# Layer 0 of a two-layer attention block: output product over two rows by seven products, inverses spread by transfers, gate by tanh

## The chip, the cores and the metric

The kernel runs on one core of one Trainium2 chip. The metric is the device time of one execution in microseconds (us). Everything is computed in fp32.

The engines are named as in the profile: PE (TensorE, the matmuls; PEld is its loading of the stationary operand), DVE (VectorE), ACT (ScalarE), POOL (GpSimd) and SP (SyncE, which here only issues DMA transfers). PE writes to PSUM, eight banks of 512 fp32 columns on 128 partitions.

## The reference

Two layers, each of which normalizes its input by groups of channels and adds an attention to it. The input `x` is 1 x 128 x 256 x 256: 128 rows (`S`), in each 256 places (`R`) with 256 channels (`C`). The change is in layer 0, whose core is:

```python
gate = sigmoid(msa_repr @ gate_proj)                       # msa_repr = gn(x)
q, k, v = split(msa_repr @ qkv_proj, 3)                    # 8 heads of 32 channels
sim = softmax(einsum('nsqhc,nskhc->nshqk', q, k) * 32 ** -0.5)
sim = sim + bias                                           # bias from pair_repr, the same for all rows
attend = einsum('nshqk,nskhc->nsqhc', sim, v) * gate
x = x + attend @ out_proj
```

Attention runs inside each of the 128 rows. Layer 1 is a banded attention with 4 heads of 64 channels; `x` between the layers is kept in DRAM (`x1`). The statistics that layer 1's normalization needs are gathered while layer 0 produces its rows.

## The kernel before, in words

Channels lie on the partitions, in two halves of 128. A tile of one row is [128, 2 halves, 256 places]. An early stage of some 190 us loads `x` for the statistics, turns the pair tensor into `bias_sb` and prepares weights. Layer 0 is then one loop over the rows `s`. Layer 1 follows.

**Two rows at a time by seven products.** Two rows times two halves of channels against a 2 x 2 block of weights would be eight products of 128 x 128 by 256 columns. `Seven` does it with seven, in Strassen's manner: `Quarters` holds the sums of weight quarters, `row_sums` (on POOL) makes sums of the normalized rows in `ts`, and the products are added on top of each other inside a PSUM bank, so that a half bank must be read between two products: product 7 is added to the half bank after ACT has copied it (`take("6")`), and product 4 after `take("7")`. q, k, v and g (the gate's input) of two rows are made this way. `two_of_them` runs two of them interleaved: q and k in an even iteration, v and g in an odd one. A product is four matmuls on strips of 32 columns of the array, and each of these has two records in the trace.

**The output product** is done row by row with all eight products per two rows: `one_by_one` yields after each of its four products per row, and `two_of_them` takes one from this generator (`next(po, None)`) behind product 7 of the first, one behind product 4 of the first, and the other two at the end. In iteration `s` it works on row `s - 1`.

**One iteration `s`** (the text calls it even or odd by `s`), in the order of the program:

- `scores(s, 0)`: scores of the first four heads into four banks, four exponentials on ACT (`ex`);
- `sum_heads(s - 1)`: the softmax totals `zs` of the row before, as products of ones with `both` (the sum of both halves of the keys, added by `join_tiles` on DVE), a head's total lying on 32 partitions, 512 columns in all; then `bv`, the product of bias and values;
- `divide(s - 1)`: ACT copies `zs` to `z` (and adds it up in `zsum`), DVE makes `d = (g + 1) * z` and its reciprocal. `g` holds exp(-gate input), made by ACT in every even iteration for two rows;
- `attend(s - 1)`: `av`, the product of exponentials and values; on DVE `t = bv * z`, `t = av + t`, `at = t * d`;
- `scores(s, 1)`, three exponentials, then `stretch`: the two `Seven` with the output product between them, and the fourth exponential behind the first copy;
- the remaining joins, `least` (the minimum of `z`), `normal(s + 4)` (transposes and normalizes a later row), `sum_rows` in odd iterations, `finish(s - 1)` (adds `xt` to the output product, statistics, the store of two rows).

PE, ACT and DVE run in exactly this order in layer 0 (a manual schedule); POOL and SP are ordered by the planner.

**PSUM.** Five of the eight banks are one ring for scores, `Seven`, `two` and the output product; a new use takes the bank that was given back longest ago. `zs`, `bv` and `av` have one bank each.

**Layer 1** makes its output product by seven already (`Summed`) and spreads its inverses by transfers: `by_transfer` writes them to DRAM (`rz_far`) and reads them back broadcast over partitions (`near`).

Of the kernel before, what the change touches and what calls it, by code (L numbers as in the profile page):

```python
# [15 lines left out]
P = 128  # L16
# [23 lines left out]
def conv_preact_kernel(  # L40
# [103 lines left out]

    w_out_t = const.tile([P, 2, C], F32, name="w_out_t")
# [35 lines left out]
    quarters["g"] = Quarters(const, gate_sb, 0, "g")  # L181

# [178 lines left out]
    with ExitStack() as early:  # L361
# [10 lines left out]
        def load_weights():  # L372
            w_raw = pr_pool.tile([P, 8, C], F32, tag="pr", name="w_raw")
            nc.gpsimd.dma_start(out=w_raw[:, 6:8, :], in_=out_w.rearrange("(t p) c -> p t c", p=P))
            nc.gpsimd.dma_start(out=w_raw[:, 0:6, :], in_=w_in.rearrange("(t p) c -> p t c", p=P))
            nc.gpsimd.dma_start(out=w_nat[:, 6:8, :], in_=w_out.rearrange("(t p) c -> p t c", p=P))
            nc.gpsimd.dma_start(out=b_raw[0:6], in_=b_in.rearrange("(t p) -> t p", p=P))
            nc.gpsimd.dma_start(
                out=b_raw[6:8].rearrange("h (a r) -> h a r", a=A),
                in_=b_out.rearrange("(a h r) -> h a r", a=A, h=2),  # L380
            )
            for h in range(2):
                cols = slice(h * P, (h + 1) * P)
                for to, t0, t1 in ((out_sb, 6, 8), (w_nat, 0, 6)):
                    nc.gpsimd.tensor_copy(
                        to[:, 0 : t1 - t0, cols].rearrange("p t (a r) -> p t a r", a=A),
                        w_raw[:, t0:t1, :].rearrange("p t (a h r) -> p t h a r", a=A, h=2)[:, :, h],
                    )
# [177 lines left out]
    def row_sums(t, x, engine):  # L566

        engine.tensor_tensor(t[:, 0], x[:, 2], x[:, 0], ALU.subtract)  # L568
        engine.tensor_tensor(t[:, 1], x[:, 3], t[:, 0], ALU.subtract)
        engine.tensor_tensor(t[:, 2], x[:, 3], x[:, 2], ALU.subtract)  # L570
        engine.tensor_tensor(t[:, 3], x[:, 1], t[:, 1], ALU.subtract)
# [51 lines left out]
    def two_of_them(pool, f, g, name, po, rest=lambda: None):  # L623


        for p in (f, g):
            p.open()
            p.product(1)
            p.product(5)
            p.take("15")  # L630
            if p is f:
                rest()
        twos = proj_bank(f"p2{name}")
        two = pool.tile([P, 2, R], F32, tag="two", name=f"two{name}", bufs=1)
        f.product(2, twos[:, 0, :], first=True)
        g.product(2, twos[:, 1, :])
        nc.scalar.copy(two, twos)  # L637
        for p in (f, g):
            p.product(3)
            p.product(6)  # L640
            p.take("6")

        for n, what in ((7, "7"), (4, "34")):
            f.product(n)
            f.take(what)
            next(po, None)
            g.product(n)
            g.take(what)
        for _ in po:
            pass  # L650
        for n, p in enumerate((f, g)):
            p.add_two(two[:, n, :])
            p.add_mid()
# [41 lines left out]

    def in_turn(sevens, amid=lambda n: None):


        for p in sevens:
            p.open()  # L700

            p.product(2, p.ps[:, 1, :], first=True)
            p.take(2)
        for n in (1, 5, 6, 7, 4, 3):
            for p in sevens:
                p.product(n)
                p.take(n)
            if n in (1, 5):
                amid(n)
# [22 lines left out]
    with ExitStack() as both:  # L732
# [6 lines left out]
        ygs = {}  # L739
        rz_far = dram.tile([2, 2, 4, R], F32, name="rz_far")  # L740

        def load1(g):
            if g * XG < S and g not in ygs:

                if g % 7 < 2:
                    yg = big.tile([P, XG * (R // B), C // A], F32, tag="xg", name=f"yg{g}")
                    yg = yg.rearrange("p n c -> p (n c)").rearrange("p (s h q) -> p s h q", h=2, q=R)
                else:
                    yg = big1.tile([P, XG, 2, R], F32, tag="yg", name=f"yg{g}", bufs=5)
                nc.sync.dma_start(out=yg, in_=rows(x1, g * XG, XG))  # L750
                ygs[g] = yg

        with ExitStack() as lay0:
# [6 lines left out]
            xns, tss, res = {}, {}, {}  # L760

            def normal(s):
# [5 lines left out]
                xt = row.tile([P, 2, R], F32, tag="xt", name=f"xt{s}", bufs=6)  # L768
# [63 lines left out]
            def sum_heads(s):  # L832
# [4 lines left out]
                for half in range(2):  # L837
                    both = hd[s, half][1]
                    for j in range(4):
                        nc.tensor.matmul(  # L840
                            zs[D0 * j : D0 * (j + 1), half, :], lhsT=ones[:, 0:D0], rhs=both[:, j, :],
                            start=True, stop=True,
# [5 lines left out]
            def divide(s, zs):  # L848
                if s < 0:
                    return  # L850
                i, r = divmod(s, 2)
                z = att.tile([P, 2, R], F32, tag="z", name=f"z{s}", bufs=1)
                nc.scalar.activation(z, zs, AF.Identity, accum_out=zsum[:, s : s + 1])
                d = att.tile([P, 2, R], F32, tag="d", name=f"d{s}", bufs=1)
                nc.vector.scalar_tensor_tensor(d, res["g", i][:, 2 * r : 2 * r + 2, :], 1.0, z, op0=ALU.add, op1=ALU.mult)
                nc.vector.reciprocal(d, d)  # L856
                hd[s, "z"] = (z, d)

            def least(s, z):
                if s >= 0:  # L860
                    nc.vector.tensor_reduce(zmin[:, s : s + 1], z, axis=AX.XY, op=ALU.min)

            def attend(s):
# [5 lines left out]
                z, d = hd.pop((s, "z"))  # L869
                t = att.tile([P, 2, R], F32, tag="t", name=f"t{s}", bufs=1)  # L870
                nc.vector.tensor_tensor(t, bv0, z, ALU.mult)  # L871
                nc.vector.tensor_tensor(t, av, t, ALU.add)
                at = row.tile([P, 2, R], F32, tag="at", name=f"at{s}", bufs=1)
                nc.vector.tensor_tensor(at, t, d, ALU.mult)  # L874
                st[s]["at"] = at

            def finish(s):
                if s < 0:
                    return
                po = st[s]["po"]  # L880
                g, k = divmod(s, XG)
                if k == 0:
                    outs[g] = big1.tile([P, XG, 2, R], F32, tag="o", name=f"o{g}")
                o = outs[g]
                nc.vector.tensor_tensor(o[:, k], po, st[s]["xt"], ALU.add)
                first, part = (k, S // 2 - 1 + k) if s >= S - 2 else (k - 1, s // 2)
                if first == k or k == 1:
                    for half in range(2):
                        nc.vector.bn_stats(out=stats1[:, half, part, :], in_=o[:, first : k + 1, half, :])
# [3 lines left out]
                st.pop(s)  # L893

            def stretch(names, i, s, rest=lambda: None):

                po = iter(())
                if s >= 0:
                    po = one_by_one(out_sb, st[s]["at"], f"po{s}", lambda ps: st[s].update(po=ps), B)
                if 2 * i >= S:  # L900
                    rest()
                    for _ in po:
                        pass
                    return
# [8 lines left out]
            with tc.manual_schedule(engines={mybir.EngineType.PE, mybir.EngineType.Activation, mybir.EngineType.DVE}):  # L913
# [3 lines left out]
                stretch("qk", 0, -1)  # L917
                for s in range(2, 4):
                    normal(s)
                stretch("vg", 0, -1)  # L920
                sum_rows(1)
                most1 = Most(st1, stats1, 3, 1)
                for s in range(S):
                    scores(s, 0)()
                    zs = sum_heads(s - 1)
                    join_tiles(s, 0, 0)
                    divide(s - 1, zs)
                    if s % 2 == 0:
                        e = res["g", s // 2]
                        nc.scalar.activation(e, e, AF.Exp, scale=-1.0)  # L930
                    z = hd[s - 1, "z"][0] if s > 0 else None
                    rest = ((0, 2), (1, 0), (1, 2))
                    if s < S - 1:
                        attend(s - 1)
                        last_exp = scores(s, 1)
                        if s == 4:
                            for weights in quarters1.values():
                                weights.sum()
                        stretch(("qk", "vg")[s % 2], s // 2 + 1, s - 1, last_exp)
                        for half, j in rest:  # L940
                            join_tiles(s, half, j)
                        least(s - 1, z)
                        if s >= S - 3:
                            most1.join(s - S + 3)
                        normal(s + 4)
                        if s % 2 == 1:
                            sum_rows((s + 3) // 2)
                        finish(s - 1)
                    else:

                        scores(s, 1)()
                        for half, j in rest:
                            join_tiles(s, half, j)
                        least(s - 1, z)
                        attend(s - 1)
# [11 lines left out]
                attend(S - 1)  # L967
                for s in (S - 2, S - 1):
# [12 lines left out]
        with ExitStack() as lay:  # L981
            ps_av = psum(lay, "1", 4, 0)
            row = lay.enter_context(tc.tile_pool(name="row1", bufs=4))
# [368 lines left out]
    with tc.If(sure < P):  # L1352
        with ExitStack() as lay:
# [69 lines left out]
            def again(layer, s, mean, rstd):  # L1423
# [38 lines left out]
                if layer == 0:  # L1462
# [5 lines left out]
                    nc.vector.tensor_tensor(at, at, e, ALU.mult)  # L1468
# [64 lines left out]
```

## Time and profile before

| What | Value |
|---|---|
| Time, median of 3 runs | 3140.39 us (3139.83 to 3141.06) |
| The profiled execution's own time | 3144.71 us |
| Its span, first to last instruction | 3142.9 us |
| Granted PE clock, mean | 0.993 |
| PE busy | 3062.3 us, 97% |
| DVE busy | 2542.5 us, 81% |
| ACT busy | 1869.8 us, 59% |
| POOL busy | 1623.3 us, 52% |
| Layer 0 in the trace | from about 190 us to about 2065 us |

The profile is of one execution, so its durations are to be compared with its own time; the median of the runs is 4.3 us lower. Engines overlap, so the shares do not add up. A line such as `L577` is a line of the kernel; `out<-in` names the tiles; `[idle <- X]` is how long the engine stood before the instruction, and what released it. In the answer by stretches, each line has the stretch, its length, then busy time (and instructions) of PE, PEld, DVE, ACT and POOL, the granted clock, the DMA share and GB/s.

### The profile page before, as it was taken

How to read it: one execution, taken by the hardware profiler on the slowest of the kernel's cores; microseconds unless marked ns; L12 is line 12 of the kernel's file. 1: busy time of each engine (PE TensorE's matmuls, PEld its weight loads, DVE VectorE, ACT ScalarE, POOL GpSimd, SP SyncE). 2: the span in 40 equal slices, each digit the busy share in tenths (PEclk: the TensorE clock that was granted, in tenths of full speed). 3: DMA queues.
4: the chain of work that ended last, by engine and by line, in shares of the span. 5: the costliest groups of instructions: out<-in, count | busy, mean ns of one | idle time of the engine just before them, and what ended most of it. 6: DMA issues, size and time to landing. Idle time of an engine off the chain costs nothing.

```text
span 3142.9 us, 135072 instructions
## 1 busy us (share of the span) xinstructions
PE 3062.3 (97%) x60161; PEld 2030.7 (65%) x60161; DVE 2542.5 (81%) x4140; ACT 1869.8 (59%) x4064; POOL 1623.3 (52%) x1651
## 2 busy tenths in 40 slices
PE   6889999999999999999999999999999999999997
PEld 4556666566666656666665666567777777777775
DVE  4669999999999999999999999956666666666665
ACT  4666666666666666666666666645555555555553
POOL 3034444444444444444444444347677777777774
PEclk9999999999999999999999999999999999999999
DMA  9941111111111111111111111004444444444443
GB/s 376 424 122 42 44 43 36 43 37 41 38 36 43 36 43 37 42 37 36 43 36 43 37 41 38 30 29 103 100 100 103 95 98 104 101 99 102 95 99 70
DMA packets 357293, 245.47 MB, mean 78 GB/s; under 512 B 276072, under 2 KB 342112, under 8 KB 350560
## 3 DMA queue, kind: packets, MB, share of 16 engines
q1 hardware_dynamic: 355808, 234.39, 27.4%
q8 instruction: 474, 7.77, 1.1%
q0 software_dynamic: 752, 2.36, 0.2%
q14 instruction: 115, 0.94, 0.1%
q10 hardware_dynamic: 144, 0.00, 0.0%
HBM read 169.09 MB, written 67.62 MB: 75 GB/s over the span
## 4 chain that ended last, share of the span: by engine, by line
PE 91%; DMA 5%; DVE 2%; ACT 1%; issue 0%; POOL 0%; SPq 0%; DVEq 0%; POOLq 0%; ACTq 0%
PE sim L794 8%; PE po L577 7%; PE av L826 7%; PE bv L826 7%; PE p1v L1055 7%; PE p1q L577 6%; PE p1o L577 6%; PE p1k L577 6%; PE pv L577 6%; PE pq L577 6%; PE pk L577 5%; PE pg L577 5%; DMA pr<-in_L_conv_pair_repr_dram 4%; PE zs L840 4%; PE 1sim L1076 3%; PE 1av L1117 3%
## 5 line engine op out<-in xcount | busy, mean ns | idle before, releaser
L807 ACT ACTIVATE ex<-sim 128x512 f32<-128x512 f32 x1024 | 547.6, 605 | 422.4 <-PE sim L794 422.4
L816 DVE TENSOR_TENSOR both<-ex 128x512 f32<-128x512 f32 x512 | 487.7, 991 | 69.1 <-ACT ex L807 68.9
L856 DVE RECIPROCAL d<-d 128x512 f32<-128x512 f32 x128 | 429.2, 3353 | 4.4
L618 POOL TENSOR_TENSOR v<-v,twovg 128x256 f32<-128x256 f32 x64 | 78.4, 1224 | 544.4 <-ACT twovg L637 544.4
L577 PE MATMUL po<-at,out_sb 128*32 128x256 f32 x4096 | 291.6, 381 | 4.1 <-DVE at L874 4.1
L794 PE MATMUL sim<-q,k 32*64 32x256 f32 x8192 | 288.3, 387 | 1.2 <-ACT ex L807 1.2
L826 PE MATMUL bv<-bias_sb,v 128*32 128x256 f32 x4096 | 244.5, 379 | 0.7 <-DVE t L871 0.7
L826 PE MATMUL av<-ex,v 128*32 128x256 f32 x4096 | 244.5, 379 | 0.0
L1086 POOL TENSOR_TENSOR 1p<-1ex,seen 128x768 f32<-128x768 f32 x127 | 231.8, 1825 | 13.0 <-ACT 1ex L1084 13.0
L1055 PE MATMUL p1v<-w_in_t,1xn 128*64 128x128 f32 x4096 | 236.4, 273 | 0.3 <-POOL place L990 0.3
L1055 PEld LDWEIGHTS p1v<-w_in_t,1xn 128*64 128x64 f32 x4096 | 231.6, 137 | 6.0 <-POOL place L990 0.6
L677 ACT ACTIVATE 1q<-p1q,bqk 128x256 f32<-128x256 f32 x192 | 91.1, 474 | 242.5 <-PE p1q L577 126.4
L794 PEld LDWEIGHTS sim<-q,k 32*64 32x64 f32 x8192 | 152.1, 131 | 126.8 <-issue 79.2
L618 POOL TENSOR_TENSOR q<-q,twoqk 128x256 f32<-128x256 f32 x64 | 51.8, 810 | 290.7 <-ACT twoqk L637 290.7
L1186 DVE TENSOR_TENSOR 1at<-1av,1near 128x512 f32<-128x512 f32 x128 | 82.5, 686 | 143.2 <-DMA 1near<-rz_far 124.2
L826 PEld LDWEIGHTS bv<-bias_sb,v 128*32 128x32 f32 x4096 | 133.2, 110 | 88.7 <-issue 1.1
L826 PEld LDWEIGHTS av<-ex,v 128*32 128x32 f32 x4096 | 133.2, 110 | 87.9 <-issue 0.4
L577 PEld LDWEIGHTS po<-at,out_sb 128*32 128x32 f32 x4096 | 131.2, 110 | 70.8 <-issue 4.7
L1093 POOL TENSOR_TENSOR 1zp<-1p 128x512 f32<-128x512 f32 x127 | 162.4, 1279 | 10.0
L568 POOL TENSOR_TENSOR 1ts<-1xn 128x256 f32<-128x256 f32 x64 | 46.8, 732 | 230.6 <-ACT 1xn L1016 230.6
L775 DVE TENSOR_SCALAR xn<-xt,mean,rstd 128x256 f32<-128x256 f32 x256 | 160.8, 667 | 0.0
L334 DVE BATCH_NORM_STATS2 stats<-xs 128x6 f32<-128x128 f32 x512 | 100.3, 277 | 65.1 <-DMA xs<-in_x_dram 65.1
(300 smaller groups left out, 7599.0 us busy)
## 6 DMA issues: line engine op xcount, KB each, us to landing
pr<-in_L_conv_pair_repr_dram SPq DMA_DIRECT2D x32, 1024.0 KB
xs<-in_x_dram SPq DMA_DIRECT2D x16, 2048.0 KB
x<-o SPq DMA_DIRECT2D x64, 512.0 KB
yg<-x SPq DMA_DIRECT2D x64, 512.0 KB
out_dram<-1o SPq DMA_DIRECT2D x256, 128.0 KB
xg<-in_x_dram SPq DMA_DIRECT2D x252, 128.0 KB
1near<-rz_far SPq DMA_DIRECT2D x124, 256.0 KB
rz_far<-1rz SPq DMA_DIRECT2D x124, 4.0 KB
```

Source lines behind the costliest of these rows:

```text
L577: nc.tensor.matmul(out[cols], lhsT=lhsT[:, cols], rhs=rhs, **flags)
L618: nc.gpsimd.tensor_tensor(self.to[:, 0], self.to[:, 0], two, ALU.add)
L775: nc.vector.tensor_scalar(xns[i][:, 2 * r + half, :], xt[:, half, :], mean0[:, half : half + 1], rstd0[:, half : half + 1], op0=ALU.subtra ...
L794: nc.tensor.matmul(sims[j][KB * c : KB * (c + 1), kt, :], lhsT=k[p0 : p0 + D0, 2 * r + half, k0 : k0 + KB], rhs=q[p0 : p0 + D0, 2 * r + ha ...
L807: nc.scalar.activation(ex[:, j], sims[j], AF.Exp, scale=1.0 / math.sqrt(D0))
L816: nc.vector.tensor_tensor(both[:, j : j + 2], ex[:, j : j + 2, 0, :], ex[:, j : j + 2, 1, :], ALU.add)
L826: nc.tensor.matmul(to[D0 * j : D0 * (j + 1), half, :], lhsT=v[:, 2 * r + half, c0 : c0 + D0], rhs=weights(4 * half + j, kt), start=(kt == ...
L840: nc.tensor.matmul(zs[D0 * j : D0 * (j + 1), half, :], lhsT=ones[:, 0:D0], rhs=both[:, j, :], start=True, stop=True,)
L856: nc.vector.reciprocal(d, d)
L1055: nc.tensor.matmul(ps[KB * half : KB * (half + 1), b, :], lhsT=xns[i][:, 2 * r + kt, KB * b : KB * (b + 1)], rhs=w_in_t[:, kt, 2 * C + P * ...
L1086: engine.tensor_tensor(p.rearrange("p j (r c) -> p (j r) c", c=WROW)[:, :, 0 : 2 * WSTEP] .rearrange("p r (t c) -> p r t c", c=WSTEP)[:, : ...
L1093: engine.tensor_tensor(zp, p[:, :, 0:R], p[:, :, R : 2 * R], ALU.add)
```

## The change

- The output product of layer 0 goes over two rows by seven products (`Output`, a `Summed`). It works on rows `s - 3` and `s - 2` in odd iterations `s`; even iterations have none. Its operand `at` is kept for two rows, POOL makes the row sums (`out_sums`), and DVE takes each product's result, adding `xt` on the way. `two_of_them` asks for the output products at more places.
- The totals of both halves of the heads are packed into 256 columns (16 partitions each, by `place0`). DVE takes the reciprocal of these 256 columns. One transfer writes eight partitions of it to DRAM, four read it back, each broadcast over 32 partitions (`near`). The last row does this by two products with `spread0` instead.
- The row's result is `at = (tanh + 1) * (av * near + bv)` in three DVE steps (`gated`), at the end of an even iteration, and between the takes of the output product in an odd one; `av` and `bv` stay in PSUM until then. ACT makes tanh of half the gate's input where it made the exponential, and `out_sb` is halved when it is loaded.
- The order in an iteration: the fourth exponential of the first heads comes behind `divide`; `join_tiles(s, 0, 2)`, `least` and `normal(s + 4)` come before `scores(s, 1)`.
- `row_sums` does two of its four subtractions in one instruction (in both layers). `xt` has eight buffers instead of six; layer 1's `yg` buffers are allocated only in layer 1.

```diff
     def row_sums(t, x, engine):
-        engine.tensor_tensor(t[:, 0], x[:, 2], x[:, 0], ALU.subtract)
+        engine.tensor_tensor(t[:, 0::2], x[:, 2:4], x[:, 0::2], ALU.subtract)
         engine.tensor_tensor(t[:, 1], x[:, 3], t[:, 0], ALU.subtract)
-        engine.tensor_tensor(t[:, 2], x[:, 3], x[:, 2], ALU.subtract)
         engine.tensor_tensor(t[:, 3], x[:, 1], t[:, 1], ALU.subtract)
...
-        for p in (f, g):
-            p.product(3)
-            p.product(6)
-            p.take("6")
-
-        for n, what in ((7, "7"), (4, "34")):
-            f.product(n)
-            f.take(what)
-            next(po, None)
-            g.product(n)
-            g.take(what)
+        f.product(3)
+        next(po, None)
+        f.product(6)
+        f.take("6")
+        next(po, None)
+        g.product(3)
+        next(po, None)
+        g.product(6)
+        g.take("6")
+        f.product(7)
+        f.take("7")
+        next(po, None)
+        g.product(7)
+        g.take("7")
+        f.product(4)
+        f.take("34")
+        next(po, None)
+        g.product(4)
+        g.take("34")
         for _ in po:
             pass
...
+    class Output(Summed):
+        WIDTH = B
...
+        def out(self, to, half, m, r):
+            nc.vector.tensor_tensor(to, self.ps[:, half, :], self.y[r][:, m], ALU.add)
+
+        def stream(self, amid=()):
+            amid = iter(amid)
+            self.open()
+            for n in (2, 1, 5, 6, 7, 3, 4):
+                if n == 2:
+                    self.product(2, self.ps[:, 1, :], first=True)
+                else:
+                    self.product(n)
+                self.take(n)
+                next(amid, lambda: None)()
+                yield
...
                     for j in range(4):
                         nc.tensor.matmul(
-                            zs[D0 * j : D0 * (j + 1), half, :], lhsT=ones[:, 0:D0], rhs=both[:, j, :],
-                            start=True, stop=True,
+                            zs[strip(j), 0, :], lhsT=place0[:, half, :], rhs=both[:, j, :],
+                            start=(half == 0), stop=(half == 1),
                         )
...
-                z = att.tile([P, 2, R], F32, tag="z", name=f"z{s}", bufs=1)
-                nc.scalar.activation(z, zs, AF.Identity, accum_out=zsum[:, s : s + 1])
-                d = att.tile([P, 2, R], F32, tag="d", name=f"d{s}", bufs=1)
-                nc.vector.scalar_tensor_tensor(d, res["g", i][:, 2 * r : 2 * r + 2, :], 1.0, z, op0=ALU.add, op1=ALU.mult)
-                nc.vector.reciprocal(d, d)
+                z = att.tile([P, R], F32, tag="z", name=f"z{s}", bufs=1)
+                nc.scalar.activation(z, zs[:, 0, :], AF.Identity, accum_out=zsum[:, s : s + 1])
+                rz = att.tile([P, R], F32, tag="rz", name=f"rz{s}", bufs=1)
+                nc.vector.reciprocal(rz, zs[:, 0, :])
+                near = att.tile([P, 2, R], F32, tag="near", name=f"near{s}")
+                if s < S - 1:
+                    far = rz0_far[s % 2]
+                    nc.sync.dma_start(out=far.rearrange("j h q -> (j h) q"), in_=rz[0 : P : B // 2])
+                    for j in range(A):
+                        nc.sync.dma_start(
+                            out=near[strip(j)].rearrange("p h q -> p (h q)"),
+                            in_=far[j].rearrange("h q -> (h q)").partition_broadcast(B),
+                        )
...
-                nc.vector.tensor_tensor(t, bv0, z, ALU.mult)
-                nc.vector.tensor_tensor(t, av, t, ALU.add)
-                nc.vector.tensor_tensor(at, t, d, ALU.mult)
+                    lambda: nc.vector.tensor_tensor(t, av, near, ALU.mult),
+                    lambda: nc.vector.tensor_tensor(t, bv0, t, ALU.add),
+                    lambda: nc.vector.scalar_tensor_tensor(
+                        at, res["g", i][:, 2 * r : 2 * r + 2, :], 1.0, t, op0=ALU.add, op1=ALU.mult
+                    ),
...
                 for s in range(S):
-                    scores(s, 0)()
+                    last_exp = scores(s, 0)
                     zs = sum_heads(s - 1)
+                    divide(s - 1, zs)
                     join_tiles(s, 0, 0)
-                    divide(s - 1, zs)
+                    last_exp()
                     if s % 2 == 0:
                         e = res["g", s // 2]
-                        nc.scalar.activation(e, e, AF.Exp, scale=-1.0)
+                        nc.scalar.activation(e, e, AF.Tanh, scale=0.5)
...
+                    attend(s - 1)
+                    join_tiles(s, 0, 2)
+                    if s > 0:
+                        least(s - 1, hd[s - 1, "z"][0])
+                    normal(s + 4)
+                    last_exp = scores(s, 1)
...
+                    late = [lambda j=j: join_tiles(s, 1, j) for j in (0, 2)]
+                    if s % 2 == 1 and s > 1:
+                        i = (s - 3) // 2
+                        out_sums(i)
+                        po = output(i, gated(s - 1))
+                        first, late = [last_exp] + late, []
+                    else:
+                        po = iter(())
+                        first = [last_exp]
+                        late += gated(s - 1)
...
+                    if s < S - 2:
+                        stretch(("qk", "vg")[s % 2], s // 2 + 1, po, rest)
+                    else:
+                        rest()
+                        for _ in po:
+                            pass
+                    for work in late:
+                        work()
```

## The prediction

> **What bounds the kernel now.** I read the page's first table, then the busy time by stretches, then the chain of work that ended last in two windows, then single engines' timelines.
>
> ```profile
> PE 3062.3 (97%) x60161; PEld 2030.7 (65%) x60161; DVE 2542.5 (81%) x4140; ACT 1869.8 (59%) x4064; POOL 1623.3 (52%) x1651
> ```
> PE is busy 97% of the span. The edit lives in layer 0, so its stretch counts:
> ```profile
> 1200.00:1400.00 200.00, 200.00 (x4380) 122.31 (x4376) 187.34 (x222) 129.22 (x269) 90.18 (x83) 1.00 0.16 40
> ```
> There PE (first column) is never idle, at full granted clock, and DVE (third) is busy 187 of 200 us. PE sets the pace: an iteration takes 14.49 us (first scores at 1202.24, the next at 1216.73). Less work on DVE, ACT or POOL buys nothing; PE work removed does, if PE stays without gaps. Whether it does is decided by what stands between dependent products. The chain in an even iteration of today (q and k):
> ```profile
> 1227.81 0.43 PE pq L577 x8
> 1228.24 0.43 PE po L577 x8
> 1228.67 0.43 PE pk L577 x8
> 1229.10 0.43 PE pq L577 x8
> 1229.54 0.43 PE po L577 x8
> ```
> Product 7 of q, an output product, 7 of k, 4 of q, an output product: 0.43 us each, nothing between. The output products fill the time in which ACT copies a half bank out before the next product adds onto it. Iteration 0 has no output product yet, and shows the same q and k products without them:
> ```profile
> 214.57 0.91 PE pk L577 x16
> 215.48 0.02 issue
> 215.50 0.38 ACT midk L611
> 215.88 0.04 issue
> 215.93 0.64 PE pk L577 x8
> 216.56 0.52 PE pq L577 x8
> 217.09 0.61 PE pk L577 x8
> 217.70 1.19 PE sim L794 x32
> ```
> ACT's copy is now a link of the chain. From 215.48 to the end of the next scores at 218.89 it takes 3.41 us. Four products at 0.432 and scores at 1.05 would take 2.78. So 0.63 us are lost where no output product covers.
>
> **Output product.** Per two rows it goes from eight products to seven: -0.432 us of PE per pair. But all seven stand in the odd iteration; `po` of an even one is empty. Every even iteration then runs as iteration 0 did: the order of products 3, 6, 7, 4, their copies and the banks (scores take over what q's copy frees) are the same. +0.63 us per pair. This row decides the sign: +0.20 per pair before anything else.
>
> **Odd iterations.** The seven are put singly between v and g products, so those stay covered. New is that each output product adds onto a half bank that DVE must have read. Positions are counted from the first scores, on the trace's odd iteration (1202.24). Product 3 of v starts at 9.18 (1211.42); output product 2 follows at 9.61, is done 0.61 later and read 0.07 after that, as the rows of these products and copies show: 10.3. Is DVE free then? Its reciprocal starts at about 2.2; then 1.75 (layer 1's 64 columns take 0.55, 128 take 0.95, so 256: 0.95 + 2 x 0.40), two joins at 0.99, the minimum 0.41, two transposes 0.76, two normalizations 1.33, two joins: 10.4. Just in time. From there DVE has take 2, multiply by `near`, take 1, add `bv`, take 5, gate, take 6 in order. A take is priced by layer 1's like operation:
> ```profile
> 2408.64 0.42 DVE L684 TENSOR_TENSOR 1q<-p1q,1q 128x256 f32<-128x256 f32 x1
> ```
> The 512-column steps take 0.69 (lines 872, 874). Start to start that is 0.41+0.65+0.41+0.68+0.41+0.69, and take 6 ends 0.42 later: 10.3+3.67 = 13.97; PE starts 0.2 after a release (midv done 1212.97, product 1213.16). Output product 7, which overwrites what take 6 reads, has its turn at 9.18 + 11 x 0.432 = 13.93 and so waits 0.24. If the gate step goes at the mean of today's like step (line 855, 0.90), 0.45; at 1.13, as in the even iteration of this window, 0.68. Lower bound 0, if DVE overlaps more. I take 0.35, between the first two, which are the nearest rows. Of the other such waits, output product 4 behind take 7 just fits (14.3+0.68+0.42+0.2 against 14.3+3 x 0.432); the rest have 0.4 us or more to spare.
>
> **Inverses by transfer.** The 512-column reciprocal (3.35 us) and the step before it (0.90) leave DVE; 256 columns, one write of 8 KB and four reads of 64 KB per row come. PE is not waiting for that DVE work today, so the gain is nothing; the price is a new wait of `near`, behind which stand takes 1, 5 and 6 on DVE and so PE. Layer 1 does the same per pair:
> ```profile
> 2411.74 1.09 SPq L1162 DMA_DIRECT2D rz_far<-1rz  x2
> 2413.38 1.12 SPq L1166 DMA_DIRECT2D 1near<-rz_far  x2
> ...
> 2418.13 1.29 DVE L1186 TENSOR_TENSOR 1at<-1av,1near 128x512 f32<-128x512 f32 x2 [1.71 <-DMA 1near<-rz_far]
> ```
> The write is followed after 1.64 us; the second read (issued 2413.96) is in after 4.07, with four times the bytes of one here. Reciprocal done at 3.95, write in at 5.6, four issues about 0.57 apart, the last at 7.3, landing 1.64 (a small transfer) to 4.07 later: 9.0 to 11.4. It is needed at 10.7. Late by 0 to 0.7; I take 0, since 64 KB is nearer the small end. In even iterations DVE has some 3 us to spare before the next reciprocal.
>
> The Trainium skill, "DMA: Bandwidth & Descriptors", advises under "Rules for kernel authors" to coalesce small transfers, as under 64 KB one pays mostly overhead, which speaks against these; its "Anatomy of one DMA" gives about 2.0 us fixed cost. By that (an estimate) `near` would be in at 3.95 + 2.0 + 1.7 + 2.0 = 9.7, in time; the rows' 4.07 is twice that, and the bound keeps it.
>
> **What costs nothing, and what hides it.** The totals still take eight matmuls of 256 columns into a 32-row strip each: 0.86 us of PE as now. ACT's copy of them halves (0.63 to about 0.40, line 1197); the fourth exponential moves behind it, done near 4 where it is needed at 6.55. The tanh has the shape of today's exponential (1.06 us); in the even iteration that ended at 1222.32, 1.1 us before the second scores arrived: a tenth of a us more would not show, a table change would. POOL gets `out_sums` (1.28+0.73+0.73 = 2.7 us per pair) at 45% busy: free at 1.6, done at 4.4, needed at 11.3; else product 5 waits. SP issues five more transfers per row, 2.6 of 14.5 us; its stores and `x` loads behind them are ordered rows ahead. `bv` and `av` stay in their banks to the end of the iteration (13.6 of 16), wanted again 2 and 4 us into the next. Layer 1's `yg` buffers now wait for layer 0's memory, some 20 us before ACT reads the third (2089.6). Halved weights and constants: at the start, beside loads.
>
> **Ends.** Iteration 1 loses four products and their cover: -1.73+0.63 = -1.1. In iteration 126 the chain today runs 6.3 us through DVE (2031.4 to 2037.7) before the output products; these go. In iteration 127 the seven come bare, about +5; the last row's reciprocal saves 1.6, its product and copy of `near` add 1.5. I take -2, from -8 to +4.
>
> **Sum.** 62 pairs x (-0.43+0.63+0.35) = +34; -1.1; -2: +31 us. The profiled execution took 3144.7 (span 3142.9, 1.8 around it), so 3176; the median shown is 3140.4, 4.3 below it, so **3171**. By odd wait: 0 gives 62 x 0.20 - 3 = +9, 3150; 1.3 (0.6 and `near` 0.7 late) gives 62 x 1.50 - 3 = +90, 3230.
>
> **Rivals.** (a) *PE stays full*: the seventh product saved is all that counts. 62 x -0.43 - 3 = -30, 3110: faster. For it: PE has no gap now. Against: iteration 0. It decides if the even gaps fall below 0.43 us with no odd wait. 6%. (b) *Even gaps alone*: DVE keeps up in the odd iterations, and the end gains more: 3134 to 3149, middle 3145. For it: DVE loses 1.9 us of work per iteration (7.6 us of today's steps for d, inverse, attend, minimum and sum against 5.7). 14%. (c) *Transfers late*: `near` at 11.4 or later, behind `x` loads: 3205 to 3230. For it: DVE waits for it in layer 1 (1.71 us above). Against: there it is asked for sooner. 10%. (d) *Tanh needs its own table*: the only load shown in layer 0 (1.28 us, before the first exponential) would come twice per pair; 2.57 less 1.1 of slack, 1.5 us x 64 = +94 on top: 3265. 3%.
>
> "ScalarE: Activation LUTs" of the Trainium skill, "Table sets", has tanh in exp's set, so no load and (d) void; no run here shows a tanh.
>
> My forecast, both gaps: 67%, alone 3150 to 3205. A measurement can tell about 0.2%, 6 us: below 3134 is (a), 3134 to 3147 most of (b). Faster 0.06, same 0.10, slower 0.84. The range 3145 to 3210 leaves out (a), (d), half of (c) and part of (b).
>
> **What would show it.** Right: PE's busy time about 27 us less in layer 0 and the span longer; waits of PEld pq, pk for ACT midq, midk about 62 times each; scores after k's product 4 without output products; output product 7 waiting for DVE's mid. Wrong: a pair of iterations under 28.98 us, which would overturn the even gap; waits of DVE for DMA `near`, then (c); ACT table loads in layer 0, then (d).

## The result and the profile after

The changed kernel takes 3371.8 us (median of four, 3364.7 to 3376.3) against 3140.5 for the kernel before: 1.073 times as long [1.072, 1.075], 231 us. It is slower, as forecast, but the forecast was 31 us, and 3371.8 lies far outside its range of 3145 to 3210. The profiled execution took 3371.2, with a span of 3369.5.

The first table of the changed kernel's page:
```profile
PE 3143.4 (93%) x59661; PEld 2009.3 (60%) x59661; DVE 2094.2 (62%) x4327; ACT 1835.9 (54%) x4065; POOL 1623.2 (48%) x1660
```
Its stretch from 1200 to 1400 us, in the columns of before (PE, PEld, DVE, ACT, POOL, granted clock, DMA share, GB/s):
```profile
1200.00:1400.00 200.00, 185.94 (x3904) 107.50 (x3904) 124.67 (x219) 112.92 (x242) 80.81 (x86) 1.00 0.19 53
```
PE has 500 matmul records fewer, about eight for each of the saved products. Yet in layer 0 it now stands idle 14 of 200 us, where it never did. DVE, at 187 of 200 us before, is down to 125. All five engines have room: what sets the pace is a chain of waits between them. The chain that ended last runs through both kinds of iteration (start, length, what):
```profile
1203.70 1.96 DMA near<-rz_far
...
1206.39 0.43 DVE o L705
1206.82 0.14 issue
1206.95 0.64 PE po L590 x8
...
1210.73 0.68 PE po L590 x8
1211.41 0.02 issue
1211.44 0.44 DVE o L715
1211.87 0.14 issue
1212.01 0.64 PE po L590 x8
1212.65 1.05 PE sim L843 x32
...
1223.72 0.38 ACT midk L624
1224.10 0.04 issue
1224.15 0.64 PE pk L590 x8
```
The last three rows are the forecast even gap: they repeat iteration 0 of the kernel before. The rest is new. In the odd iteration the reads of `near` stand on the path, and after them DVE's takes of output products (line 705 is take 1, line 711 take 7, line 715 take 3) alternate with the products themselves.

Periods are counted here from the first totals product of one iteration to that of the next, means over the steady part of layer 0. In the last three kernels the totals are made at another place of the iteration, so there only the pair can be compared with the rows above:

| us | even | odd | pair | time | ratio to before |
|---|---|---|---|---|---|
| before | 14.46 | 14.49 | 28.95 | 3140.5 | 1 |
| after | 13.41 | 19.12 | 32.53 | 3371.8 | 1.073 [1.072, 1.075] |
| `sp_order` | 13.41 | 17.81 | 31.22 | 3287.1 | 1.047 [1.045, 1.049] |
| `gate_last` | 13.43 | 17.70 | 31.13 | 3284.9 | 1.046 [1.044, 1.048] |
| `inverse_first` | 13.41 | 17.75 | 31.16 | 3283.9 | 1.045 [1.044, 1.047] |
| `spaced` | 13.41 | 16.19 | 29.60 | 3185.4 | 1.014 [1.012, 1.016] |
| `two_banks` | 13.41 | 15.96 | 29.37 | 3170.2 | 1.009 [1.008, 1.011] |
| `bare_even` | 13.27 | 15.87 | 29.14 | 3162.3 | 1.006 [1.004, 1.007] |
| `all_of_it` | 11.44 | 17.36 | 28.80 | 3143.2 | 1.000 [0.999, 1.001] |
| `joins_first` | 11.44 | 17.17 | 28.61 | 3122.2 | 0.994 [0.993, 0.996] |

62 pairs at 32.53 - 28.95 = 3.58 us make 222 of the 231 us. Odd iterations of the changed kernel vary from 17.68 to 21.58; in the experiments with a lower odd period most stand at one value. (Beside the experiments the kernel before took 3140.4 to 3144.6 us; each ratio is to the runs beside it.)

### The profile page after: what moved, and what is told of

Same layout as the page of the kernel before. It is cut to its first block, busy times and chain, and to the rows that moved or that the text cites. A ratio compares the mean times of both kernels' runs of the same rounds, so it can differ in the third digit from the quotient of the medians.

```text
span 3369.5 us, 135301 instructions
## 1 busy us (share of the span) xinstructions
PE 3143.4 (93%) x59661; PEld 2009.3 (60%) x59661; DVE 2094.2 (62%) x4327; ACT 1835.9 (54%) x4065; POOL 1623.2 (48%) x1660
## 4 chain that ended last, share of the span: by engine, by line
PE 69%; DVE 12%; DMA 9%; issue 3%; SPq 3%; ACT 3%; POOL 0%; DVEq 0%; ACTq 0%; POOLq 0%
PE p1v L1158 6%; PE sim L843 6%; PE p1q L590 6%; PE pk L590 6%; PE po L590 6%; PE p1k L590 5%; PE p1o L590 5%; DMA near<-rz_far 5%; PE pq L590 5%; PE zs L889 4%; PE av L875 3%; PE bv L875 3%; DVE rz L903 3%; SPq L909 3%; PE 1sim L1179 3%
## 5 line engine op out<-in xcount | busy, mean ns | idle before, releaser
L856 ACT ACTIVATE ex<-sim 128x512 f32<-128x512 f32 x1024 | 564.1, 606 | 527.7 <-PE sim L843 527.7
L903 DVE RECIPROCAL rz<-zs 128x256 f32<-128x256 f32 x128 | 225.0, 1758 | 323.9 <-ACT z L901 323.9
L865 DVE TENSOR_TENSOR both<-ex 128x512 f32<-128x512 f32 x512 | 350.1, 704 | 120.8 <-ACT ex L856 112.9
L634 POOL TENSOR_TENSOR v<-v,midv 128x512 f32<-128x512 f32 x64 | 81.8, 1279 | 329.0 <-ACT v L628 329.0
L843 PEld LDWEIGHTS sim<-q,k 32*64 32x64 f32 x8192 | 164.6, 131 | 124.3 <-issue 78.7
L590 PE MATMUL po<-att,sums_o 128*32 128x256 f32 x1512 | 129.0, 404 | 88.0 <-DVE o L705 86.9
L631 POOL TENSOR_TENSOR v<-v,twovg 128x256 f32<-128x256 f32 x64 | 46.6, 728 | 340.3 <-ACT twovg L650 332.6
L582 POOL TENSOR_TENSOR 1ts<-1xn 128x512 f32<-128x512 f32 x64 | 81.5, 1274 | 234.9 <-ACT 1xn L1119 234.9
L944 DVE TENSOR_TENSOR t<-av,near 128x512 f32<-128x512 f32 x128 | 88.5, 692 | 134.0 <-DMA near<-rz_far 121.4
L1165 ACT COPY 1v<-p1v 128x512 f32<-128x512 f32 x128 | 75.1, 587 | 124.9 <-PE p1v L1158 124.9
```

The lines of the kernel that those rows point to most:

```text
L590: nc.tensor.matmul(out[cols], lhsT=lhsT[:, cols], rhs=rhs, **flags)
L843: nc.tensor.matmul(sims[j][KB * c : KB * (c + 1), kt, :], lhsT=k[p0 : p0 + D0, 2 * r + half, k0 : k0 + KB], rhs=q[p0 : p0 + D0, 2 * r + ha ...
L856: nc.scalar.activation(ex[:, j], sims[j], AF.Exp, scale=1.0 / math.sqrt(D0))
L865: nc.vector.tensor_tensor(both[:, j : j + 2], ex[:, j : j + 2, 0, :], ex[:, j : j + 2, 1, :], ALU.add)
L903: nc.vector.reciprocal(rz, zs[:, 0, :])
```

## Experiments

My theory after reading the two traces: two causes share the loss of the odd iterations. First, an output product waits for the take before it even where that take reads the other half of the bank. Second, `near` is late, so that its multiply on DVE holds back take 1, and with it product 5 and all that is queued behind on PE. The rivals: the second alone, with everything behind it merely shifted; or the even gap being much larger than its rows. For the lateness itself three causes were open: the order on SP, the order of the steps on DVE, and the late start of the reciprocal.

**SP in written order** (`sp_order`). In the changed kernel SP's order is the planner's. SP's queue there (start, length, what):
```profile
1199.27 0.57 SPq L907 DMA_DIRECT2D rz_far<-rz  x1
1201.60 0.34 SPq L369 DMA_DIRECT2D xg<-in_x_dram  x1
1202.03 2.10 SPq L909 DMA_DIRECT2D near<-rz_far  x4
```
The `x` load of line 369 stands ahead of the reads of `near`; by the chain it is issued only after DVE's transposes of the row whose place it takes and the `xn` at 1201.57. The edit writes SP's order out as well:
```diff
-            with tc.manual_schedule(engines={mybir.EngineType.PE, mybir.EngineType.Activation, mybir.EngineType.DVE}):
+            with tc.manual_schedule(engines={mybir.EngineType.PE, mybir.EngineType.Activation, mybir.EngineType.DVE, mybir.EngineType.SP}):
```


> The changed kernel, with SP's instructions of layer 0 kept in the order of the program, so that the load of a later x no longer stands between the write of the inverses and their reads. Theory 1 (near comes late because of what stands ahead of it on SP): in odd iterations near comes 1.0 to 1.6 us sooner, the odd iteration falls from 19.3 to 17.6-18.3 us, and the clock dips behind the long waits go; 62 x 1.0 to 1.7 = 60 to 105 us less, 3265 to 3310 us. Theory 2 (the odd iteration is long because each output product waits for DVE's take of the one before it, also when it adds onto the other half of the bank): no change, 3365 to 3376.

Measured: 3287.1, 85 us less. Its SP queue:
```profile
1154.10 0.57 SPq L907 DMA_DIRECT2D rz_far<-rz  x1
1155.78 2.24 SPq L909 DMA_DIRECT2D near<-rz_far  x4
```
Reads start 1.68 us after the write here, 2.76 with the `x` load between; over the odd iterations the medians are 1.68 and 2.72 (2.57 to 3.66 in the changed kernel). The odd iteration falls to 17.68 in its median, and no further.

**Gate steps behind the takes** (`gate_last`). The multiply by `near` and the two steps after it no longer stand amid the takes:
```diff
-                        po = output(i, gated(s - 1))
-                        first, late = [last_exp] + late, []
+                        po = output(i, ())
+                        first, late = [last_exp] + late, list(gated(s - 1))
```


> The changed kernel, with the three gate steps of an odd iteration behind all takes of the output product, so that nothing PE needs stands behind the wait for near. Theory 1 alone (only the late near costs): the odd iteration falls to 15.8 us, 62 x 3.5 = 215 us less, 3156. Theory 2 alone (only the takes, one after the other, cost): no change, 3372. Both, as I read the trace: the waits between output products stay, 0.30+0.36+0.31+0.85 = 1.8 us per odd iteration, which comes to 17.6 us; 62 x 1.7 = 105 us less, 3255 to 3285.

Measured: 3284.9, again 17.68 for most odd iterations. In odd iterations nothing waits for `near` now, and what is left are waits between products and takes. PE's timeline (the bracket: idle time before, and what ended it):
```profile
1155.13 0.62 PE L590 MATMUL pv<-sums_v,ts 128*32 128x128 f32 x16
1155.86 0.64 PE L590 MATMUL po<-at,out_sb 128*32 128x256 f32 x8
...
1157.13 0.64 PE L590 MATMUL po<-att,sums_o 128*32 128x256 f32 x8 [0.21 <-DVE o L705]
...
1160.16 0.64 PE L590 MATMUL pg<-ts,gate_sb 128*32 128x256 f32 x8
1160.91 0.64 PE L590 MATMUL po<-at,sums_o 128*32 128x256 f32 x8
1162.19 0.64 PE L590 MATMUL po<-att,out_sb 128*32 128x256 f32 x8 [0.64 <-DVE o L715]
```
These are product 1 behind one of v, product 5, then 3 behind one of g, and 4. Product 5 writes half 1 and waits for take 1, which reads half 0; product 4 writes half 0 and waits for take 3, which reads half 1. Against the spacing of products of 0.43, four output products start late, by 0.30, 0.40, 0.31 and 0.85: 1.86 us. They are products 1, 5 and 3, which have one other product between them and the output product before, and product 4, which has none. Products 6 and 7, with two between, start on time.

**Reciprocal ahead of ACT's copy** (`inverse_first`). Both read the totals from one bank, and in the changed kernel the reciprocal waited for the copy, and the copy stood behind three exponentials. The waits of the changed kernel from 300 to 2000 us (total, times, longest):
```profile
DVE rz L903 <- ACT z L901: 265.2, 104, 4.3
...
DVE t L944 <- DMA near<-rz_far: 101.3, 82, 2.4
```
```diff
-                nc.scalar.activation(z, zs[:, 0, :], AF.Identity, accum_out=zsum[:, s : s + 1])
                 nc.vector.reciprocal(rz, zs[:, 0, :])
+                nc.scalar.activation(z, zs[:, 0, :], AF.Identity, accum_out=zsum[:, s : s + 1])
```


> The changed kernel, with DVE's reciprocal of the totals ahead of ACT's copy of them in the program. In the changed kernel the reciprocal waits for ACT's copy, which stands behind three exponentials, and starts 3.1 to 3.25 us after the iteration's first scores. If that wait is only the order of two readers of one bank, it starts at about 2.2, near comes 0.95 us sooner, and the odd iteration falls by 0.9 or, with fewer clock dips, by 1.3: 3290 to 3320 us. If near's reads are held by what stands ahead of them on SP, whatever the reciprocal does, the gain is under 0.3 us per odd iteration: 3352 to 3372. Theory 2 alone: no change.

Measured: 3283.9, better than expected. The wait between the two readers is turned round, as ACT's timeline shows (lines 901 and 903 have changed places):
```profile
1152.69 0.38 ACT L903 ACTIVATE z<-zs 128x256 f32<-128x256 f32 x1 [1.32 <-DVE rz L901]
```
So two reads of one bank do wait for each other in this program, whichever stands first. SP's `x` load, which might have held the reads all the same, did not: with the earlier write the reads stood ahead of it (1154.31 and 1156.93 in one iteration).

Each of these three edits alone takes the odd iteration to the same 17.68. No run combines two of them alone, but as each ends at the same value, their gains should not add: each removes nearly all that the late `near` cost PE, 1.4 us per pair, and the waits between products and takes stay. The rival that `near` alone explains the loss is refuted, since without it 1.7 us per pair are still there.

**Output products spread** (`spaced`). The seven go between the products of v and g so that two others stand between any two of them, and the joins and gate steps go amid the takes:
```diff
             if p is f:
                 rest()
+            next(po, None)
...
         nc.scalar.copy(two, twos)
+        next(po, None)
         f.product(3)
-        next(po, None)
         f.product(6)
         f.take("6")
         next(po, None)
         g.product(3)
-        next(po, None)
...
+                        po = output(i, late + [idle, idle] + list(gated(s - 1)))
```


> The changed kernel, with the output products of an odd iteration spread over the whole stretch, two other products between any two of them, DVE's last two joins and the gate steps moved between the takes to where they fall due (the gate steps behind the fifth, sixth and seventh take). Theory 2: with 1.3 us between output products the waits for takes go; left is about 0.6 us before the next scores (only one product behind k's or g's last), so odd iterations take about 16.4 us, 62 x 2.9 = 178 us less, 3180 to 3215. Theory 1 alone: near has the same time as with the gate steps last, so this is no faster than that kernel.

Measured: 3185.4, 186 us less, and 99 less than `gate_last`, which also takes the gate steps out of PE's way. Its chain in an odd iteration:
```profile
1175.59 0.43 PE po L590 x8
1176.03 0.44 PE pv L590 x16
1176.46 0.43 PE pg L590 x8
1176.89 0.43 PE po L590 x8
```
An output product every 1.30 us, and no take in the chain. In the changed kernel a take and the product that waits for it are 1.28 us (1210.73 to 1212.01); with one product between two of them, 0.86 apart, they can't keep up, and with two they do.

**Halves in two banks** (`two_banks`). Like `gate_last`, in the changed kernel's own order of products, but each half of the output product has a bank of its own, and so product 5 opens one:
```diff
+        def open(self):
+            self.ps = Halves([proj_bank(f"p{self.name}_{half}") for half in range(2)])
...
-                    self.product(n)
+                    self.product(n, first=n == 5)
```


> The changed kernel with the gate steps last, as in gate_last (odd iteration 17.8 us), and with one edit more: the two halves of the output product lie in two banks of the ring instead of one, in the same order of products. My prediction took it that a product waits only for a take from the half that it writes. If the program makes it wait for any take from the same bank, then two banks restore what I assumed: product 1 no longer waits for take 2, nor 5 for take 1, nor 3 for take 7, and the odd iteration falls from 17.8 to 16.0-16.3 us (the next scores wait some 0.3 us for the second bank): 62 x 1.5 to 1.8 = 95 to 110 us less than gate_last, 3175 to 3195 us. If each output product waits for the take before it for another reason (DVE's order, the sums on POOL), nothing changes: 3285.

Measured: 3170.2, 115 us less than `gate_last`, 1.74 us per odd iteration; 5 us better than expected. On PE's timeline the last output product, which had waited 0.64 us, follows 0.44 after the one at 1111.93, and none waits:
```profile
1112.37 0.61 PE L590 MATMUL po<-att,out_sb 128*32 128x256 f32 x8
```
The takes, their order and durations are the same; only whose bank they read is changed. So the 1.74 us come from two halves sharing a bank, not from DVE's order or POOL's sums. Each half is here also a tile of its own, and no run separates the tile from the bank; that two reads of one bank waited for each other speaks for the bank.

**All of it** (`all_of_it`), and the same without cover, that is without other products in the gaps, in even iterations (`bare_even`). On top of `spaced`: SP in written order, the reciprocal first, the totals moved to the end of the iteration, the normalization of a coming row to the start, and in even iterations totals and bias-by-value products put between the bare last products of q and k:
```diff
+            def both_of(s):
+                yield from totals(s)
+                yield from biased(s)
...
         f.product(7)
         f.take("7")
+        fill()
         g.product(7)
         g.take("7")
         next(po, None)
+        fill()
         f.product(4)
         f.take("34")
+        fill()
...
-                        first = [last_exp]
-                        late += gated(s - 1)
+                        first = [last_exp, join[0]] + gate + [join[1]]
```
`bare_even` gives the two-product function an empty cover:
```diff
-                        stretch(("qk", "vg")[s % 2], s // 2 + 1, po, rest, now)
+                        stretch(("qk", "vg")[s % 2], s // 2 + 1, po, rest, iter(()))
```


> Everything the first four kernels point to, in one: output products of an odd iteration with two others between any two; totals made at the end of an iteration instead of behind the next scores, the reciprocal at once and ahead of ACT's copy; SP in the order of the program; gate steps between the takes at places where near is in; and in even iterations the two products of the totals and three of bias by values put between and behind products 7 and 4 of q and k, where an output product stood before. If the waits named so far are all there is, both iterations run without gaps: 28.96 - 0.43 = 28.5 us per pair, 62 x 0.43 = 27 us under the kernel before, 3105 to 3120. If the transfers, wherever they start, still hold DVE, or product 1 waits for the take in the now shorter odd iteration: 0.2 to 0.6 us more per pair, 3125 to 3150.

> The same, except that in even iterations nothing stands between products 7 and 4 of q and k: the totals come behind k's product 4, bias by values behind the next scores. Only the cover is taken away. By the price of iteration 0 (0.25 before k's 7, 0.09 before q's 4, 0.18 before k's 4; the wait of the next scores stays covered by the totals) an even iteration takes 0.5 us longer than in the kernel with cover: 62 x 0.5 = 32 us more than it. If the cover does not matter, both take the same.

Measured: 3143.2, above the 3105 to 3120 for no further wait and inside the 3125 to 3150 for transfers that still hold DVE, and 3162.3. The cover is worth 19 us instead of the 32 forecast, because `all_of_it` has a wait of its own. In a third of its pairs DVE stood as in this timeline:
```profile
986.02 0.69 DVE L966 TENSOR_TENSOR t<-av,near 128x512 f32<-128x512 f32 x1 [0.49 <-DMA near<-rz_far]
...
988.52 1.22 DVE L872 TENSOR_TENSOR both<-ex 128x512 f32<-128x512 f32 x1
```
The multiply waits for `near`, the last gate step behind it takes 1.13 us here instead of 0.69, the last join stands behind both, and the second totals product, used as cover, behind the join: its weight load at 989.79 waits 0.46 us for that join. What makes `near` late there stays open: in this pair one of its four reads took 1.32 us to issue, the others 0.30 to 0.42, but in other such pairs all four were issued in the usual time, and `x` loads follow the reads on SP in the pairs without the wait too. `bare_even`, whose totals come later, has no such wait.

**Joins ahead of the gate steps** (`joins_first`). That wait removed, and in the last iteration, which has no v and g, the cover put between the output products:
```diff
-                        first = [last_exp, join[0]] + gate + [join[1]]
+                        first = [last_exp] + join + gate
...
                         for _ in po:
-                            pass
+                            next(cover, None)
```


> all_of_it with two edits. In even iterations both last joins come ahead of the gate steps on DVE: in all_of_it one of them stands behind the wait for near, and where near is late (x loads on the DMA engines at that time) the second product of the totals waits 0.6 us, in about a third of the pairs. And in the last iteration the totals and bias by values go between the bare output products. If that wait is what all_of_it lacks, every pair takes 28.61 us: 62 x 0.35 = 21 us under the kernel before in layer 0, 2 us lost at the end; ratio 0.993 to 0.996. If near is late enough to hold DVE beyond the join too, the ratio stays at 0.998 to 1.000.

Measured: 3122.2, 0.994 [0.993, 0.996] of the kernel before, 19 us faster than it and 250 faster than the change. Its chain in an even iteration:
```profile
1214.17 0.43 PE pq L590 x8
1214.60 0.43 PE zs L898 x8
```
Totals products stand where the kernel before had output products. Totals and bias-by-value products go on so between the later ones, and PE is busy 200.00 of 200 us from 1200 to 1400 again. The pair is 28.61, against 28.95 - 0.43 = 28.52 with one product less and no gap anywhere. Against `bare_even`, which doesn't have that wait either, the cover is worth 0.53 us per pair.

## Why the prediction was right in sign and wrong in size

The pair of the changed kernel, term by term, each from a difference of two runs: 28.95 before; -0.43 for the saved product; +0.68 for the even gap (13.41 against 14.46 less four products of 0.432); +0.17 left over in the odd iteration of `two_banks` (15.96 against 14.49 plus three products; its scores behind the last output product take 1.29 where they took 1.12); +1.74 for the bank waits (`gate_last` less `two_banks`); +1.42 for `near` (after less `gate_last`). The sum is 32.53, as measured.

- **Saved product**, -0.43: right.
- **Even gap**, forecast 0.63: 0.68. Here 0.54 of it lies between the products and 0.14 in the scores after them, which wait for the bank that q's copy frees. The row of iteration 0 decided the sign, as the prediction said.
- **Odd waits on banks**, forecast 0.35, measured 1.74: the step that failed is that an output product waits only for the take of its own half. "Output product 7, which overwrites what take 6 reads" was counted as the waiter; in `gate_last` product 7 starts on time, and the waits stand at products 1, 5, 3 and 4, of which the prediction said that 4 "just fits" and "the rest have 0.4 us or more to spare". Each of the four comes right behind a take of the other half. A rule of the Trainium skill that I missed would account for such waits. "PSUM — Partial Sum Buffer", "PSUM bank collisions raise a hardware error", says to guard the accumulators by bank and 32-row quadrant, not by address, since two engines in the same quadrant of one bank at once collide, two readers included. The traces agree that this program waits so: 1.74 us per pair went away with the second bank. No run here shows a collision. The same rule would explain the reciprocal's wait for ACT's read of the same bank: with the copy behind it (`inverse_first`) it starts 1.14 us after the first totals product instead of 2.06. The 265 us that DVE stood before it are not all the copy's, though: in `inverse_first` DVE still stands 204 us before it, now for the totals themselves.
- **`near` late by 0**, measured 1.42 per pair: the prediction has the multiply by `near` due 10.7 us after the first scores. In the changed kernel it starts at 12.2 (median of the odd iterations), in `inverse_first` at 10.6. Three assumptions failed. The reciprocal was to start about 2.2 us after the first scores; it started at 3.1 to 3.3, behind ACT's copy. The prediction had SP's "stores and `x` loads behind them are ordered rows ahead"; one `x` load stood in front and held the reads 1.1 us (2.76 against 1.68 after the write). And take 1, which stands behind the multiply, held product 5, of the other half, and not only product 6, which comes later and is the first to write the half that take 1 reads; so the rest of the output product moved with it. The durations themselves were right: 1.76 for the reciprocal (forecast 1.75), and from the last issue to the multiply that waits 2.0 to 3.9, median 2.2 (forecast for the landing 1.64 to 4.07). The 2.0 us that the prediction takes from "Anatomy of one DMA" of the Trainium skill is given there for transfers that GpSimd issues; these are issued by SP, and the shortest of them agree with it.
- **Rivals.** (c), late transfers, named the right mechanism at 10%, "behind `x` loads", and its sign, waits of DVE for `near`, came (101 us in the list above), but it priced `near` alone at 3205 to 3230; the measured 1.42 x 62 = 88 us on top of the forecast would have been 3259. (d) is out: the changed kernel has five activation table loads, at 2.1, 184.7, 206.7, 2284.6 and 2308.5 us, none in the layer's iterations, where exponential and tanh alternate. (a) and (b) fell with the even gap and the odd waits.
- **Ends**, forecast -1.1 and -2: iteration 1 takes 13.41 instead of 14.49, as forecast. From the totals of iteration 126 to the end the kernel before took 1114.4 us, the changed one 1121.6. Iteration 126 gained 5.4 us (8.3 from totals to totals instead of 13.7), but iteration 127, with seven bare output products, takes 22.2 where it took 5.5; 4.1 us come back after it. "About +5" for the bare products was the step that failed. The bank waits are only a part of it: the same iteration takes 24.8 in `gate_last` and still 18.6 in `two_banks`. In the changed kernel product 1 waits 2.67 us for take 2, which stands behind DVE's joins, the product of bias and values waits 2.73 for a gate step behind `near`, and after these waits the granted clock is 0.50 from 2260 to 2263 us and 0.51 from 2270 to 2278.

The forecast of 3171 is within 1 us of `two_banks`, the kernel in which the halves don't wait for each other and nothing that PE needs waits for `near`. That is partly luck: `two_banks` loses 0.17 in the odd iteration, at the scores and not at product 7, where the forecast had 0.35, and 0.68 in the even one, where it had 0.63. The sum came out near for that kernel; the waits in the changed one were other ones.

## To carry to other kernels

When a product and the read of its sum alternate on one accumulator bank, count the link (here 1.28 us for read, release and next product) against the spacing of the products, and count it for every read of that bank, whichever half it touches; put enough other products between, or give each half its own bank. Before a product that fills a gap is removed or moved, look for a place where the program already runs without it, as iteration 0 did here, and find other work to take its place. A transfer that a chain depends on is as late as the last thing ahead of it in its issuing queue: look at what that queue holds and what each entry there waits for.

## What the hardware showed beyond expectation

A wait of PE of some 2 us was at times followed by half-paced products. Two stretches of 3 us of the changed kernel (columns as above, the granted clock third from last):
```profile
1003.00:1006.00 3.00, 0.93 (x16) 0.28 (x11) 1.09 (x3) 0.24 (x1) 0.78 (x2) 1.00 0.87 188
1006.00:1009.00 3.00, 2.93 (x48) 2.23 (x52) 1.84 (x4) 0.74 (x2) 0.00 (x0) 0.70 0.09 15
```
Output product 5 waited 2.14 us there, until 1006.07. From about 1007 the products start 0.85 us apart instead of 0.43, for some 3.4 us, at a granted clock of 0.70 in this stretch and 0.73 in the next. "TensorE: Matmul & The Clock Gate" of the Trainium skill, under "HAM oscillation — how this bites in real kernels", gives the rule that idle gaps over about 3.4 us are to be avoided; here a shorter gap was followed by the lower clock already. Not every such gap was: PE waited 2.14 us from 842.9 too, and the clock was 1.00 in the 3 us from 846. From 300 to 2000 us PE waited 38 times for more than 1.1 us, up to 2.42; seven of these waits, of 1.68 to 2.42 us, were followed by such a stretch, and others as long as 2.20 were not. Over the whole run the mean granted clock was 0.987, and 0.992 in `sp_order`, where odd iterations wait less: 0.013 x 3369.5 - 0.008 x 3284.2 = 17.5 us, so an estimate of 0.3 us per pair of the 1.42 that `near` cost is lost clock. What exactly in the wait lowers the clock was not tried.
